# Attention and ternary MLP in one kernel: the comparison of the weights moved to Pool and ScalarE, the weights loaded earlier, and unread matrix passes in the first seam

## The chip, the cores and the metric

The kernel runs on one core of a Trainium2 chip. A core has TensorE (PE, the matrix engine; its weight loads are shown as PEld), VectorE (DVE), ScalarE (ACT), GpSimd (POOL) and SyncE (SP), each with its own queue of instructions that it works off in order, and 16 DMA engines, which take the transfers that SP and ScalarE issue. The metric is the time of one execution on the device in microseconds (us). Less is better.

## The reference

The input `x` is 32 sequences of 256 tokens with 128 features. One layer of attention and one gated MLP follow, each with a residual and a layer norm:

```python
scores = einsum('bhid,bhjd->bhij', Q, K) / sqrt(8)          # 16 heads of 8
scores = where(j > i, -inf, scores) - (i - j)               # causal, with a linear decay
x = layernorm(x + softmax(scores) @ V @ Wo.T + bo)
h = silu(x @ w1.T * s1) * (x @ w2.T * s2)                   # 128 -> 512
h = gelu(h @ h1.T * sh1); h = gelu(h @ h2.T * sh2)          # 512 -> 512 -> 512
x = layernorm(x + h @ w3.T * s3)                            # 512 -> 128
```

All of it is float32. The weights of the MLP (`w1`, `w2`, `h1`, `h2`, `w3`) are random -1, 0 or 1, times 8. There are about 0.7 million of them, in 11 blocks of 128 x 512.

## The kernel before

**Pairs and steps.** The 32 sequences are worked off as 16 pairs (512 tokens each). `step(n)` (line 725) weaves three things into one stream: the attention of pair n, the score maxima of pair n+1, and (from step 1 on) the MLP of pair n-1. PE, DVE, ACT and SP keep the order in which the Python program calls them (`InOrder`, line 50), so the order of the lines is the order on each engine. POOL's instructions are placed by the scheduler.

**Projections and stacks.** `project(n)` (line 314) transposes `x`, and makes queries and keys. Each is kept as a rounded half and a rest (`halves`, line 295): ACT writes `qhi`, `khi` from PSUM in the fast matmul type, DVE writes `qlo`, `klo`. Eight transfers of 256 KB (`stack`, line 305: four for q, four for k) put these halves into the rows of `qs` and `ks`, so that one matmul over 62 or 64 rows gives a score with the precision of both halves, the decay and the causal cut. I call the eight transfers stack n. Before, `stack(0, "k")`, `stack(1, "k")` and `stack(2, "k")` are issued by ACT (lines 690, 697, 758), all others by SP.

**Score tiles.** `row_maxima(n, i)` (line 373, i from 0 to 11) fills one PSUM tile of 128x1024 scores on PE, and DVE reduces it to maxima `m`. `maxima_to_rows` (line 408) transposes maxima (`pm`), splits them (`mhi` on ACT, `mlo` on DVE) and sends them by small transfers on SP into two more rows of `qs`. The tiles `mhi` and `mlo` have one buffer each, so the second pair of them waits until the first has been sent. `weigh(n, i)` (line 430) then makes the scores again, less their maximum, ACT takes the exponential `e`, POOL clears what lies above the diagonal (line 463), and `outputs` multiplies with the values `vaug` (`pa`). Score tiles, weigh tiles and MLP tiles share three PSUM buffers (`two`, line 289); small results share two (`work`, line 286).

**Opening and steps 0 and 1.** The constant rows of `qs` and `ks` are filled, pairs 0 and 1 are projected and stacked (lines 684 to 697), the values of pair 0 are projected (line 698, `pv` on PE, `vaug` on DVE), and `wo` is loaded by ACT. Then come the 12 score tiles of pair 0 with the values of pair 1 and the first `maxima_to_rows` in the middle (lines 710 to 717), the load of the MLP weights on SP (line 714) and of the scales (line 718), and two score tiles of pair 1 (`LEAD`, line 719). Step 0 runs the 12 weigh tiles of pair 0 beside the other ten score tiles of pair 1 and the projection of pair 2. Its tail, `rest()` (line 761), is the seam to step 1: the last outputs, the values of pair 2, `finish` (`pon`, `onT`, `po`).

**The comparison of the weights.** The MLP has a fast form for weights that the fast matmul type holds exactly, and a slow one for others. `inexact_weights` (line 622) copies each of the 11 blocks into the fast type on ACT (`near`), compares copy and original on DVE with an accumulated count (`differ`, `found`), and adds the counts with one matmul (`pcount`). One block is done in each of the first 11 tiles of step 0 (line 743). All engines load the number after step 0 and branch on it (lines 810 to 826); these inputs take the fast form.

**Waits of transfers.** In the order of the built instructions the transfers of SP and ACT share eight semaphores in turn. An issue waits until the transfer that used its semaphore before, mostly the eighth before it, has landed.

Of the kernel before, what the change touches and what calls it, by code (L numbers as in the profile page):

```python
# [17 lines left out]
P = 128  # L18
# [43 lines left out]
def tile_attn_ffn(  # L62
# [47 lines left out]

    qs = [const.tile([P, W, TOK], F32R, name=f"qs{i}") for i in range(2)]
    ks = [const.tile([P, W, TOK], F32R, name=f"ks{i}") for i in range(2)]
    sctx = ctx.enter_context(ExitStack())
    setup = sctx.enter_context(tc.tile_pool(name="setup", bufs=1))

# [69 lines left out]
    def fill(dst, nm, eng, groups=slice(0, W)):  # L185
        t, base = fills[nm]
        to = dst[:, groups, :]
        t = t.unsqueeze(1).to_broadcast([P, groups.stop - groups.start, TOK])
        if eng is act:
            act.activation(to, t, AF.Identity, bias=base)  # L190
        else:
            eng.tensor_scalar(to, t, base, None, ALU.add)
# [34 lines left out]
    for i in range(2):  # L227
# [7 lines left out]


    layers = (
        ("w1", w1T, 1, HID), ("w2", w2T, 1, HID), ("h1", h1T, KC, HID), ("h2", h2T, KC, HID),
        ("w3", w3T, KC, D),
    )  # L240
    near = {
        nm: const.tile([P, k, o], F32R, name=f"{nm}_near") for nm, _, k, o in layers
# [3 lines left out]
        sc[nm] = const.tile([P, KC], F32, name=nm)  # L246
    sc["s3"] = const.tile([P, 1], F32, name="s3")

    def load_layers(pool):
        got = {}  # L250
        for nm, src, k, o in layers:
            got[nm] = pool.tile([P, k, o], F32, name=f"{nm}_sb")
            sp.dma_start(out=got[nm], in_=src.rearrange("(k p) o -> p k o", p=P))
        return got
# [31 lines left out]
    def work(nm):  # L286
        return ps_w.tile([P, 512], F32, name=nm, tag="work")

    def two(nm):
        return ps_s.tile([P, 2, 512], F32, name=nm, tag="s")  # L290
# [4 lines left out]
    def halves(n, ps, bias, nm):  # L295
        pool = setup if n == 1 else hlp
        hi = pool.tile([P, TOK], F32R, name=f"{nm}hi_{n}", tag=f"{nm}hi")
        act.activation(hi, ps, AF.Identity, bias=bias)
        lo = pool.tile([P, TOK], F32R, name=f"{nm}lo_{n}", tag=f"{nm}lo")
        vec.scalar_tensor_tensor(  # L300
            lo, ps, bias, hi.bitcast(F32), ALU.add, ALU.subtract
        )
        return hi, lo

    def stack(n, nm, eng=sp):
        for r, part in {
            "q": ((0, 0), (1, 0), (2, 1), (3, 1)), "k": ((0, 0), (2, 0), (1, 1), (3, 1))
        }[nm]:
            eng.dma_start(
                out=pairs[n][nm][PAIRING + r :: W, :, :].bitcast(F32),  # L310
                in_=pairs[n][nm + "s"][part].bitcast(F32),
            )
# [26 lines left out]
    def project_values(n):  # L339
        xT, v = pairs[n]["xT"], vaug[n % 2]  # L340
        pairs[n]["v"] = v
        pv = work(f"pv_{n}")
        for t in range(NT):
            pe.matmul(
                pv[:, t * D : (t + 1) * D], lhsT=xT[:, t * P : (t + 1) * P], rhs=wv_sb,
                start=True, stop=True,
            )
        to = v[:, :, 0 : H // 2 * VSLOT].rearrange("p t (r c k) -> p t r c k", r=2, c=C)
        src = pv.rearrange("p (t r e c d) -> p t r e c d", t=NT, r=2, e=2, c=C)
        bias = bv_sb.rearrange("p (r e c d) -> p r e c d", r=2, e=2, c=C)  # L350
        for r in range(2):
            for e in range(2):
                vec.tensor_tensor(
                    to[:, :, r, :, 2 * e * VHEAD : 2 * e * VHEAD + HD], src[:, :, r, e],
                    bias[:, r, e].unsqueeze(1).to_broadcast([P, NT, C, HD]), ALU.add,
                )
# [265 lines left out]
    def inexact_weights():  # L622

        found = const.tile([P, 11], F32, name="found")
        at = 0
        for nm, *_ in layers:
            rows = [t[nm].rearrange("p k o -> p (k o)") for t in (loaded, near)]
            for c in range(0, rows[0].shape[1], HID):
                whole, part = (t[:, c : c + HID] for t in rows)
                act.copy(part, whole)  # L630
                differ = once.tile([P, HID], F32, name=f"differ_{at}", tag="differ")
                vec.scalar_tensor_tensor(
                    differ, whole, 1.0, part.bitcast(F32), ALU.mult, ALU.not_equal,
                    accum_out=found[:, at : at + 1],
                )
                at += 1
                yield
        ones_col = const.tile([P, 1], F32, name="ones_col")
        nc.gpsimd.memset(ones_col, 1.0)
        count = work("pcount")  # L640
        pe.matmul(count[0:1, 0:11], lhsT=ones_col, rhs=found, start=True, stop=True)
        total = const.tile([1, 1], F32, name="total")
        vec.tensor_reduce(total, count[0:1, 0:11], AX.X, ALU.add)
        number = const.tile([1, 1], I32, name="number")
        vec.tensor_copy(number, total)
        pairs["inexact"] = number
# [32 lines left out]
    def run(gen):  # L679
        for _ in gen:  # L680
            pass


    ahead = project(0)
    next(ahead)
# [2 lines left out]
    run(ahead)  # L688
    stack(0, "q", sp)
    stack(0, "k", act)  # L690
    fill(ks[1], "k", act)
    ahead = project(1)
    next(ahead)
    fill(qs[1], "q", vec)
    run(ahead)
    stack(1, "q", sp)
    stack(1, "k", act)
    project_values(0)
    for a in range(G):
        act.dma_start(  # L700
            out=wo_sb[C * HD * a : C * HD * (a + 1), :],
            in_=woT[:, :, a, :].rearrange("c d o -> (c d) o"),
        )
    sctx.close()
    ep = enter(tc.tile_pool(name="ep", bufs=5))
    op = enter(tc.tile_pool(name="op", bufs=2))
    yp = enter(tc.tile_pool(name="yp", bufs=2))
    lctx = ctx.enter_context(ExitStack())
    once = lctx.enter_context(tc.tile_pool(name="once", bufs=1))
    for i in range(6):  # L710
        row_maxima(0, i)
    project_values(1)
    maxima_to_rows(0, (0,))
    loaded = load_layers(once)
    for i in range(6, 3 * G):
        row_maxima(0, i)
    maxima_to_rows(0, (1,))
    load_scales()
    for i in range(LEAD):
# [5 lines left out]
    def step(n, exact=None, ws=None, hp=None, gp=None):  # L725


        side = iter(())
        settling = (
            last(n - 2, exact, ws, gp) if n > 1 else first_norm(0) if n else inexact_weights()  # L730
        )
        ahead = project(n + 2) if n + 2 < NPAIR else iter(())
        for i in range(3 * G):
            weigh(n, i)
            j = i + {0: LEAD, 1: -LAG}.get(n, 0)
            if n + 1 < NPAIR and 0 <= j < 3 * G:
                row_maxima(n + 1, j)
            if i == 3 and late:
                run(late.pop())
            next(side, None)  # L740
            if n and i == 9:
                turn(n - 1, exact)
            if i in ((0, 2) if n > 1 else (0, 2, 4, 6)) if n else i < 11:
                next(settling, None)

            if i in ((3, 4, 5) if n == 1 else (1, 3, 5)):
                next(ahead, None)
            if i % 3 == 2:
                run(side)
                side = outputs(n, i // 3)  # L750
            if n == 0 and i == 3 * G - LEAD:
                maxima_to_rows(1)
        if n < 2:
            run(settling)
        run(ahead)
        if n + 2 < NPAIR:
            stack(n + 2, "q")
            stack(n + 2, "k", sp if n else act)


        def rest():
            for _ in range(3):
                next(side)
                yield
            if n == 1:
                for i in range(3 * G - LAG, 3 * G):
                    row_maxima(2, i)
                    yield
            if 0 < n < NPAIR - 1:
                maxima_to_rows(n + 1)  # L770
            run(side)
            yield
            if n + 2 < NPAIR:
                project_values(n + 2)
                yield
            last_steps = finish(n)
            next(last_steps)
            yield
            yield from last_steps
            if n:  # L780
                yield
                yield from first_norm(n)
            if n == NPAIR - 1:
                yield
                turn(n, exact)
            if n > 1:
                next(settling)
                late.append(settling)

        if n:  # L790
            prepare(AF.Silu)
        due = rest()
        for _ in feed(n - 1, exact, ws, hp, gp) if n else ():
            next(due, None)
        run(due)
# [85 lines left out]
```

## Time and profile before

| what | value |
|---|---|
| time, median of 3 runs (lowest to highest) | 823.96 us (823.79 to 824.07) |
| the profiled execution's own time | 824.06 us |
| its span, first to last instruction | 822.2 us |
| PE busy | 784.6 us (95%) |
| DVE, ACT, POOL busy | 636.0, 527.5, 260.8 us |
| mean granted clock of PE | 0.98 |
| PE busy from 0 to 22 us, 22 to 42.8, 42.8 to 71, 71 to 82 | 11.71, 17.89, 26.03, 6.16 us |
| PE busy from 100 to 810 us | 703.50 of 710 us |
| DMA from 10 to 32 us | 205 to 208 GB/s, mean share of its 16 engines 0.91 to 1.00 |

A timeline row reads: start, duration, engine, line, operation, tile written <- tiles read, shapes, number of instructions merged in the row, and in brackets the idle time of the engine before it with what ended it. Most rows show line 58, because all engines but POOL are called through `InOrder`; tiles tell them apart. SPq and ACTq are issues of transfers by the queues of SP and ACT. The duration of several merged rows runs from the first start to the last end. The windows view gives for each stretch the busy time of each engine, the mean granted clock of PE (PEclk, 1.00 is full), the share of time in which the DMA engines were busy, and what they moved. The chip records the clock only from its first change on; before 32.3 us the view shows 1.00 though no record lies there, and the matmuls of the score tiles last as long (0.80 us for four) as later at 0.50.

### The profile page before, as it was taken

Reading aid. Unit: us, or ns where it says so; the run is one execution under the profiler, and the core shown is the slowest. Engines: PE = TensorE matmul, PEld = TensorE weight load, DVE = VectorE, ACT = ScalarE, POOL = GpSimd, SP = SyncE. Lnnn points to the kernel's source line nnn. Section 1 sums busy time; section 2 is a strip of 40 time slices with the busy share of each in tenths; the row PEclk is TensorE's granted clock in tenths of the full one; section 3 lists DMA queues with packets and bytes.
Section 4 is the critical chain, followed back from the end, with each engine's and each line's share of the span. In section 5 each row is a group of like instructions: output and inputs, shape, how many; then the busy total and the mean of one; then the engine's idle time right before and its main releaser. Section 6 shows DMA issues by size and latency. Waiting matters only on the chain.

```text
span 822.2 us, 17431 instructions
## 1 busy us (share of the span) xinstructions
PE 784.6 (95%) x7046; PEld 555.8 (68%) x7046; DVE 636.0 (77%) x1247; ACT 527.5 (64%) x719; POOL 260.8 (32%) x341
## 2 busy tenths in 40 slices
PE   4896999999999999999999999999999999999994
PEld 2664676776767677676767767676767767666673
DVE  6786778877887887778788877888878787873674
ACT  5065556766666766766576676667666666758572
POOL 5033413333142333414232342424243231424211
PEclk9879999999999999999999999999999999999998
DMA  6824140403204140410404040130404022000001
GB/s 147 213 62 106 29 92 14 106 15 74 60 14 106 28 107 14 92 42 21 110 17 106 27 101 20 43 90 15 107 26 104 4 62 59 14 4 14 1 8 37
DMA packets 39898, 47.49 MB, mean 58 GB/s; under 512 B 3968, under 2 KB 21632, under 8 KB 39808
## 3 DMA queue, kind: packets, MB, share of 16 engines
q1 hardware_dynamic: 37152, 42.82, 22.0%
q10 hardware_dynamic: 2656, 3.48, 1.9%
q8 instruction: 57, 0.93, 0.5%
q14 instruction: 33, 0.27, 0.1%
HBM read 7.48 MB, written 4.19 MB: 14 GB/s over the span
## 4 chain that ended last, share of the span: by engine, by line
PE 83%; DVE 4%; ACT 3%; issue 1%; DMA 0%; POOL 0%; ACTq 0%; POOLq 0%; DVEq 0%
PE peven L58 14%; PE podd L58 14%; PE s L58 12%; PE pa L58 11%; PE pw L58 10%; PE s_2d L58 2%; PE s_3d L58 2%; PE po L58 2%; PE s_0d L58 2%; PE s_1d L58 2%; PE pt L58 2%; PE pv L58 2%; PE pk L58 2%; PE pq L58 2%; PE px1T L58 1%; PE py L58 1%
## 5 line engine op out<-in xcount | busy, mean ns | idle before, releaser
L58 DVE TENSOR_REDUCE m<-s 128x4 f32<-128x1024 f32 x128 | 155.5, 1218 | 14.6 <-PE s L58 13.3
L58 ACT ACTIVATE e<-s 128x1024 f32<-128x1024 f32 x128 | 130.7, 1022 | 44.2 <-PE s L58 34.2
L463 POOL TENSOR_SCALAR_AFFINE_SELECT e<-e 128x512 f32<-128x512 f32 x128 | 82.6, 646 | 218.5 <-ACT e L58 189.3
L58 PE MATMUL podd<-h,h_near 128*128 128x512 f32 x512 | 131.3, 403 | 1.0 <-DVE m L58 0.5
L58 PE MATMUL peven<-hodd,h_near 128*128 128x512 f32 x512 | 122.7, 396 | 0.0
L58 PEld LDWEIGHTS peven<-hodd,h_near 128*128 128x128 f32 x512 | 95.7, 187 | 23.4 <-DVE hodd L58 0.3
L58 PEld LDWEIGHTS podd<-h,h_near 128*128 128x128 f32 x512 | 91.8, 188 | 23.1 <-DVE h L58 3.2
L58 ACT ACTIVATE hodd<-podd,sh 128x512 fp32r<-128x512 f32 x64 | 44.0, 688 | 62.7 <-PE podd L58 62.6
L58 PE MATMUL pw<-x1T,w_near 128*128 128x512 f32 x256 | 75.6, 418 | 1.1 <-DVE h0w L58 1.1
L274 POOL TENSOR_TENSOR rsa<-rsa,half 128x4 f32<-128x4 f32 x16 | 16.3, 1018 | 176.7 <-DVE rsa L58 176.7
L58 DVE SCALAR_TENSOR_TENSOR h0w<-pw,s,sg 128x512 f32<-128x512 f32 x64 | 47.9, 748 | 30.4 <-ACT sg L58 30.4
L58 PEld LDWEIGHTS s<-qs,ks 64*128 64x128 f32 x512 | 38.9, 188 | 47.7 <-issue 34.1
L58 PE MATMUL pa<-e,vaug 128*32 128x256 f32 x1024 | 70.6, 389 | 0.0
L58 PE MATMUL s<-qs,ks 64*128 64x256 f32 x512 | 65.3, 335 | 0.6 <-ACT e L58 0.5
L58 DVE TENSOR_TENSOR heven<-evenw,heven 128x512 fp32r<-128x512 f32 x64 | 44.2, 692 | 26.6 <-ACT evenw L58 26.1
L58 ACT ACT_TABLE_LOAD x47 | 60.3, 1283 | 3.4 <-issue 2.6
L58 ACT ACTIVATE sg<-pw,s 128x512 f32<-128x512 f32 x64 | 43.7, 684 | 28.2 <-PE pw L58 27.9
L58 PE MATMUL s<-ks,qs 62*128 62x256 f32 x512 | 56.9, 302 | 2.4 <-ACT e_0d L58 1.8
L58 ACT ACTIVATE heven<-peven,sh 128x512 fp32r<-128x512 f32 x48 | 33.4, 696 | 39.8 <-PE peven L58 39.8
L58 PEld LDWEIGHTS pw<-x1T,w_near 128*128 128x128 f32 x256 | 43.4, 188 | 18.4 <-ACT nothing L58 5.8
L581 POOL TENSOR_TENSOR h<-h0w,h 128x512 fp32r<-128x512 f32 x31 | 40.0, 1291 | 43.5 <-DVE h L58 41.2
L58 DVE TENSOR_TENSOR hodd<-oddw,hodd 128x512 fp32r<-128x512 f32 x64 | 43.7, 684 | 10.0 <-ACT oddw L58 9.9
(147 smaller groups left out, 1418.1 us busy)
## 6 DMA issues: line engine op xcount, KB each, us to landing
qs<-qhi SPq DMA_DIRECT2D x32, 256.0 KB
qs<-qlo SPq DMA_DIRECT2D x32, 256.0 KB
ks<-khi SPq DMA_DIRECT2D x26, 256.0 KB
ks<-klo SPq DMA_DIRECT2D x26, 256.0 KB
x<-in_x_dram SPq DMA_DIRECT2D x16, 256.0 KB
out_dram<-z SPq DMA_DIRECT2D x15, 256.0 KB
ks<-khi ACTq DMA_DIRECT2D x6, 256.0 KB
ks<-klo ACTq DMA_DIRECT2D x6, 256.0 KB
```

What stands on the lines that cost most here:

```text
L58: return lambda *args, **kw: self.tc.keep_in_program_order(call(*args, **kw))
L274: nc.gpsimd.tensor_tensor(rs, rs, half[:, 0:NT], ALU.pow)
L463: nc.gpsimd.affine_select(out=on_diagonal, in_=on_diagonal, pattern=[[0, on_diagonal.shape[1]], [1, P]], base=0, channel_multiplier=-1, co ...
L581: (nc.gpsimd if o < (1 if final else 2) else vec).tensor_tensor(h[:, 1, o, :], whole, h[:, 0, o, :].bitcast(F32), ALU.subtract)
```

## The change

1. *Weights loaded earlier.* `load_layers` is called right after stack 0 (before: after the first `maxima_to_rows`), in the order `w1`, `w2`, `w3`, `h1`, `h2`. On SP the five transfers (2.9 MB) now stand before the third `x` and before stack 1. The pools `ep`, `op`, `yp` and `once` are opened before the pool `setup`, so that the weights have room while it is open.
2. *Comparison on POOL and ACT.* Each block is copied by ACT as before; POOL then subtracts the copy in place, and ACT adds up the magnitudes of the rest (`Abs` with an accumulated sum), one block later. DVE only turns the 11 sums into "not zero". Three blocks are done after the projection of pair 1, two among the first six score tiles, six among the last six; the last sum stands at tile 5 of step 0, and the count (`pcount`) at tile 8.
3. *Two score tiles ahead.* Score tiles 0 and 1 of pair 0 come right after the projection of pair 1. The rests `qlo`, `klo` of pair 1 are held back (`due`) until their reduces stand in DVE's order. `project_values(0)` moves from before the score tiles to just before `project_values(1)`.
4. *Issues of ACT given to SP.* `stack(1, "k")`, the load of `wo` and `stack(2, "k")` are issued by SP.
5. *Unread passes.* `warm(4)` makes four matmuls of a 128x128 bf16 identity with 512 columns into a score buffer that nobody reads. It stands before the second `maxima_to_rows` of pair 0, and four times in the tail of step 0: after the first half of the last `pa`, after the second, after `pt`, and before `po`.

```diff
@@ line 237
-        ("w1", w1T, 1, HID), ("w2", w2T, 1, HID), ("h1", h1T, KC, HID), ("h2", h2T, KC, HID),
-        ("w3", w3T, KC, D),
+        ("w1", w1T, 1, HID), ("w2", w2T, 1, HID), ("w3", w3T, KC, D), ("h1", h1T, KC, HID),
+        ("h2", h2T, KC, HID),
@@ halves, line 300
-        vec.scalar_tensor_tensor(
-            lo, ps, bias, hi.bitcast(F32), ALU.add, ALU.subtract
+        due.append(
+            lambda: vec.scalar_tensor_tensor(lo, ps, bias, hi.bitcast(F32), ALU.add, ALU.subtract)
         )
+        if n != 1:
+            run_due()
@@ inexact_weights, line 630
+        def add_up(rest, total):
+            act.activation(rest, rest, AF.Abs, accum_out=total)
...
                 act.copy(part, whole)
-                differ = once.tile([P, HID], F32, name=f"differ_{at}", tag="differ")
-                vec.scalar_tensor_tensor(
-                    differ, whole, 1.0, part.bitcast(F32), ALU.mult, ALU.not_equal,
-                    accum_out=found[:, at : at + 1],
-                )
+                nc.gpsimd.tensor_tensor(whole, whole, part.bitcast(F32), ALU.subtract)
+                left.append((whole, found[:, at : at + 1]))
+                if at:
+                    add_up(*left.pop(0))
                 at += 1
                 yield
+        add_up(*left.pop())
+        yield
...
+        vec.tensor_scalar(found, found, 0.0, None, ALU.not_equal)
@@ new, before line 684
+    def warm(count):
+        t = two("warm")
+        for i in range(count):
+            pe.matmul(
+                t[:, i % 2, :], lhsT=ident_b, rhs=ident_b.unsqueeze(1).to_broadcast([P, NT, P]),
+                start=True, stop=True,
+            )
@@ opening, line 690
     stack(0, "k", act)
+    loaded = load_layers(once)
     fill(ks[1], "k", act)
...
     run(ahead)
+    for i in range(2):
+        row_maxima(0, i)
+    run_due()
     stack(1, "q", sp)
-    stack(1, "k", act)
-    project_values(0)
+    stack(1, "k", sp)
+    comparison = inexact_weights()
+    for _ in range(3):
+        next(comparison)
     for a in range(G):
-        act.dma_start(
+        sp.dma_start(
...
-    for i in range(6):
+    for i in range(2, 6):
         row_maxima(0, i)
+        if i > 3:
+            next(comparison)
+    project_values(0)
     project_values(1)
     maxima_to_rows(0, (0,))
-    loaded = load_layers(once)
     for i in range(6, 3 * G):
         row_maxima(0, i)
+        next(comparison)
+    warm(4)
     maxima_to_rows(0, (1,))
@@ step, line 734
             weigh(n, i)
+            if n == 0 and i == 5:
+                next(comparison)
+            if n == 0 and i == 8:
+                run(comparison)
...
-            stack(n + 2, "k", sp if n else act)
+            stack(n + 2, "k")
@@ rest, line 762
             for _ in range(3):
                 next(side)
+                if n == 0:
+                    warm(4)
                 yield
...
             next(last_steps)
+            if n == 0:
+                warm(4)
             yield
```

More of the change, by code (lines that the diff above doesn't have):

```diff
@@ L112, in tile_attn_ffn @@
     ks = [const.tile([P, W, TOK], F32R, name=f"ks{i}") for i in range(2)]
+    ep = enter(tc.tile_pool(name="ep", bufs=5))
+    op = enter(tc.tile_pool(name="op", bufs=2))
+    yp = enter(tc.tile_pool(name="yp", bufs=2))
+    lctx = ctx.enter_context(ExitStack())
+    once = lctx.enter_context(tc.tile_pool(name="once", bufs=1))
     sctx = ctx.enter_context(ExitStack())
@@ L247, in tile_attn_ffn, with load_layers @@
     sc["s3"] = const.tile([P, 1], F32, name="s3")
-    def load_layers(pool):
+    def load_layers(pool, some=layers):
         got = {}
-        for nm, src, k, o in layers:
+        for nm, src, k, o in some:
             got[nm] = pool.tile([P, k, o], F32, name=f"{nm}_sb")
@@ L299, in halves, with run_due @@
         lo = pool.tile([P, TOK], F32R, name=f"{nm}lo_{n}", tag=f"{nm}lo")
-        vec.scalar_tensor_tensor(
-            lo, ps, bias, hi.bitcast(F32), ALU.add, ALU.subtract
-        )
+        due.append(
+            lambda: vec.scalar_tensor_tensor(lo, ps, bias, hi.bitcast(F32), ALU.add, ALU.subtract)
+        )
+        if n != 1:
+            run_due()
         return hi, lo
+    due = []
+    def run_due():
+        while due:
+            due.pop(0)()
     def stack(n, nm, eng=sp):
@@ L624, in inexact_weights @@
         found = const.tile([P, 11], F32, name="found")
-        at = 0
+        at, left = 0, []
+        def add_up(rest, total):
+            act.activation(rest, rest, AF.Abs, accum_out=total)
         for nm, *_ in layers:
@@ L704, in tile_attn_ffn @@
     sctx.close()
[L705 to L709, printed above, removed]
-    for i in range(6):
+    for i in range(2, 6):
         row_maxima(0, i)
+        if i > 3:
+            next(comparison)
+    project_values(0)
     project_values(1)
     maxima_to_rows(0, (0,))
-    loaded = load_layers(once)
     for i in range(6, 3 * G):
         row_maxima(0, i)
+        next(comparison)
+    warm(4)
     maxima_to_rows(0, (1,))
@@ L729, in step @@
         settling = (
-            last(n - 2, exact, ws, gp) if n > 1 else first_norm(0) if n else inexact_weights()
+            last(n - 2, exact, ws, gp) if n > 1 else first_norm(0) if n else iter(())
         )
@@ L742, in step @@
                 turn(n - 1, exact)
-            if i in ((0, 2) if n > 1 else (0, 2, 4, 6)) if n else i < 11:
+            if i in ((0, 2) if n > 1 else (0, 2, 4, 6)):
                 next(settling, None)
```

## The prediction

> **What bounds the kernel now.** The slices and section 4 of the page say that nearly the whole span is TensorE (PE busy 95%, 83% of the chain). The change touches only what lies before that: the first 82 us. So I read stage by stage there: the timeline for what starts when, then the table of windows for the limit of each stretch. I call score tile (n,i) what `row_maxima(n, i)` makes, and weigh tile (n,i) what `weigh(n, i)` makes.
>
> The opening, in the timeline:
>
> ```profile
> 19.22 0.75 DVE L58 SCALAR_TENSOR_TENSOR qlo<-pq,bq_sb,qhi 128x512 fp32r<-128x512 f32 x1 [4.01 <-ACT qhi L58]
> ...
> 22.03 0.79 PE L58 MATMUL s<-ks,qs 62*128 62x256 f32 x4
> ...
> 22.20 0.89 DVE L58 TENSOR_TENSOR vaug<-pv,bv_sb 128x128 f32<-128x128 f32 x4 [1.57 <-issue]
> ...
> 23.13 2.36 DVE L58 TENSOR_REDUCE m<-s 128x4 f32<-128x1024 f32 x2
> ...
> 38.60 1.20 DVE L58 TENSOR_REDUCE m<-s_3d 128x8 f32<-128x1024 f32 x1
> ...
> 39.86 1.01 PE L58 MATMUL pm<-ident,m 128*8 128x128 f32 x4 [1.92 <-DVE m L58]
> ```
>
> From 23.13 to 39.80 VectorE goes from reduce to reduce, and PE waits for the last: VectorE is the limit. The work that the change puts between the reduces (`qlo`, `vaug`) stands before 23.13 here, beside idle time.
>
> The windows (columns: window; its length; PE, PEld, DVE, ACT, POOL busy; granted clock; DMA share; GB/s):
>
> ```profile
> 10.00:21.00 11.00, 5.87 (x12) 2.87 (x13) 6.07 (x7) 5.42 (x4) 5.52 (x8) 1.00 0.91 205
> ...
> 40.80:50.90 10.10, 10.10 (x81) 7.60 (x80) 8.93 (x12) 6.14 (x9) 4.47 (x7) 0.50 0.44 137
> ...
> 52.80:62.50 9.70, 9.70 (x132) 6.04 (x128) 7.93 (x15) 8.12 (x12) 3.01 (x4) 1.00 0.01 3
> 69.00:80.50 11.50, 7.67 (x78) 5.88 (x78) 4.70 (x20) 2.72 (x5) 1.38 (x2) 0.85 0.85 190
> 80.50:81.80 1.30, 0.00 (x1) 0.03 (x2) 0.53 (x1) 1.30 (x2) 1.30 (x3) 1.00 0.00 0
> 101.50:111.00 9.50, 9.50 (x72) 6.43 (x71) 7.45 (x12) 6.16 (x9) 3.67 (x3) 1.00 0.99 221
> ```
>
> Step 0 (42.8 to 71) is PE's: 10.10 of 10.10 at half clock, then 9.70 of 9.70 at full clock until 62.5. VectorE, which the comparisons load, has slack there; it holds PE only from 62.5 to 69. The seam to step 1 belongs to a transfer:
>
> ```profile
> 68.08 1.42 ACTq L58 DMA_DIRECT2D ks<-khi  x2
> ...
> 70.73 2.91 SPq L58 DMA_DIRECT2D qs<-qhi  x2
> ...
> 81.80 0.50 PE L58 MATMUL s<-ks,qs 62*128 62x256 f32 x4 [1.78 <-ACT e_0d L58]
> ```
>
> The view names `e_0d`, but that tile's buffer was not wanted. Score tile (2,0) needs all eight transfers of pair 2's stack (2.1 MB); the DMA moves 190 GB/s up to 80.5 (2.19 MB) and then nothing, and 1.3 us later the tile starts.
>
> **Opening: +1.7.** Stack 0 is 2.1 MB of the 2.26 MB moved from 10 to 21, and the third `x` shares its end, so it is there at about 21.5. I bound the first score tile by 20.2 (2.1 MB at 205 GB/s from 10.0) and today's 22.03, and take 21.5, 0.53 earlier. In the changed order two reduces precede `qlo` and `klo` of pair 1 (0.67 apart: 1.34), and pair 0's `vaug` (0.89) follows the first six reduces. All are now inside the VectorE chain: 1.34 + 0.89 - 0.53 = +1.7 at the last reduce, at `pm` and at weigh tile (0,0). It is +0.4 if the stack is early.
>
> What lies beside it: the 11 Pool subtractions have no row; the nearest is `h<-h0w,h` on Pool (128x512, 1.29 us), below it a 128x512 select (0.65), above it four 128x128 additions (4 x 0.43 = 1.7). The sums of magnitudes on ScalarE lie between 0.57 (a 128x512 copy) and 1.02 (128x1024). With 1.29 and 0.68, the chain of copies, subtractions and sums that stands before the second `mhi` on ScalarE frees it at about 42.1, and `pm` ends at about 42.5: hidden, at nothing; at 1.7 a subtraction six of them cost 2.5, some +2. Second cover: on SP's queue the weights (2.9 MB; the window from 34 to 45 moved them at 267 GB/s, 10.8 us) and the third `x` (0.26 MB, 1.0) now precede stack 1, so from 20.5 on stack 1 starts at about 32 and, at 9.5 us a stack (2.1 MB at 221 GB/s), lands at about 41.5 to 42. Score tile (1,0) wants it at 42.5; the first `mhi` and `mlo`, queued behind it, are wanted by the second `mhi` and `mlo` at the same time. Cost nothing, but each us of delay counts in full. The four passes before the second `pm` (no row; `podd` has 0.25 a 128x512 pass at full clock, 0.5 at half) take 1.0 to 2.0 and stand beside the last two reduces (2.3).
>
> **Clock: +0.85.** The granted clock changes at 35.7, 52.8, 73.3, 76.7, 83.5 and 86.9 (from its mean in short windows): always a multiple of 3.41 apart. It rises at 52.8, right after the first `pa` (50.90, 1.93 long, 128 rows). Score and weigh tiles (62 or 64 rows) kept PE busy for 10 us and did not raise it. Moved by 1.7, `pa` runs 52.6 to 54.5, past that tick, and the next is 56.2: `pq` then runs at half clock (2.04 instead of 1.12) and step 0 is at 56.4 where it was at 53.82. Bounds 0 and 1.7 (half a period).
>
> [...]
>
> **End of step 0: -1.0.** With the comparisons (11 of 0.68 to 0.80) gone from VectorE, the last reduce of pair 1 follows its tile. From 62.5 on: PE waits about 0.5 for the moved `pcount`; tile (1,11) ends at 64.25, the reduce 64.75 to 65.95 (65.48 to 66.70 before), `pm` 66.15, second-half `mlo` done 68.0 (68.93 before). SP's first stack issue goes from 70.73 to 69.75.
>
> **Seam: +0.4.** All eight transfers of stack 2 now wait on SP behind the four of the maxima; `ks` started on ScalarE's queue at 68.08 before. SP alone has a row: pair 3's stack, first issue 100.42, last bytes 110.9. Plus 1.0 until the tile starts (1.3 in the seam; 0.6 if no DMA engine lags) is 11.5 from first issue to tile; before it was 81.80 - 70.73 = 11.07. So +0.4, between 0 and +0.7. `oT` starts 1.1 earlier, without ScalarE's issues, `pv` and `po` run at full clock, and weigh tile (1,0) follows `pa` by about 5.7 (`oT` 0.65, passes 0.35 past it, `pt` 0.66, `rec` and `on` 1.3, the rest of `pv` and `vaug` 1.4, `onT` 0.69, `po` 0.6) instead of 6.9 us. That saves nothing while score tile (2,0) waits for the stack: weigh tiles and their exponentials are done about 2.5 us after (1,0), some 3 us before it. The 16 passes there (1.0 per four) lie in the same slack.
>
> [...]
>
> **Sum.** 1.7 + 0.85 - 1.0 + 0.4 = +2.0 at score tile (2,0). From there PE is the limit to the end, so it stays. The profiled execution took 824.06 (span 822.2 and 1.86 around it): 826.06; the median of the runs, 823.96, is 0.1 lower, so **826.0**. A measurement of this kernel can tell 0.2% (1.65 us) from no change.
>
> **Rivals.**
> - *Faster: the passes raise the clock at 42.6 and it holds through step 0.* VectorE is the limit then: from 43.8, 12 reduces (1.22), `xT`, `qlo`, `klo`, `rec`, `on` = 17.7, so the last reduce ends near 61.5 instead of 66.7 and stack 2 follows: -5.3, 818.7; if it holds for part of the way, 819 to 822. For: four 128-row passes and `pm` nearly fill 39.1 to 42.6. Against: before, from 32.3 to 35.7, score tiles alone let it fall again. It decides from the point where the clock is still 1.0 at 46 to 50. 0.18.
> - *Even: the opening costs nothing or the clock rises at its old tick* (stack 0 earlier than 21.5; or `pa` still in time). 2.0 - 1.3 or 2.0 - 0.85: about 824.8, down to 822. For: the clock's ticks may lie otherwise. 0.17.
> - *Slower still: stack 1 or the comparison chain ends after `pm`* (+1 to +2), or score tile (2,0) is late enough that the clock misses 86.9 (+1.7). 828 to 830. For: both covers above are under 1 us. 0.15.
> - Forecast, 824.8 to 828: 0.50, of which 0.10 lie within 0.2%.
>
> Faster by over 0.2%: 0.18 and 0.06 of the even case, 0.24. Within: 0.11 and 0.10, 0.21. Slower: 0.40 and 0.15, 0.55. The range leaves out the lower part of the first rival (0.07) and most of the last (0.13): 820.0 to 828.0.
>
> **What would show it.** First reduce near 22.6 and last of pair 0 near 41.5; clock 0.50 until 56.2; first stack issue on SP after the four maxima near 72.3; no DMA for a us before score tile (2,0) at about 83.8; from 100 us on the same table. Wrong, if VectorE has idle time before 40, if the clock is up in 44 to 52, or if score tile (2,0) starts as soon as its PSUM buffer is free.

## The result, and two profiles of the changed kernel

The changed kernel takes 826.62 us (median of 7 runs, 822.07 to 829.30) against 823.96 (823.25 to 824.53): 1.0027 times the time before, 95% interval 1.0016 to 1.0039. The forecast was 826.0.

One thing has to be read first: the profiled execution took 822.07 us, the fastest of the seven and 2.0 less than the profiled one of before. A trace of one execution can stand at the edge of the distribution. So the same kernel was profiled again (first experiment below, 826.40 us, near the median), and both traces are read here, the first as "the 822 trace", the second as "the 826 trace".

Timeline of the 822 trace, the rows that answer to those of before:

```profile
23.09 2.36 DVE L58 TENSOR_REDUCE m<-s 128x4 f32<-128x1024 f32 x2 [7.99 <-PE s L58]
...
40.76 1.20 DVE L58 TENSOR_REDUCE m<-s_3d 128x8 f32<-128x1024 f32 x1
...
42.02 1.01 PE L58 MATMUL pm<-ident,m 128*8 128x128 f32 x4
...
68.64 1.23 SPq L58 DMA_DIRECT2D qs<-qhi  x2
...
80.17 0.80 PE L58 MATMUL s<-ks,qs 62*128 62x256 f32 x4 [2.50 <-ACT e L58]
```

Timeline of the 826 trace:

```profile
22.97 2.36 DVE L58 TENSOR_REDUCE m<-s 128x4 f32<-128x1024 f32 x2 [7.90 <-PE s L58]
25.24 0.74 DVE L58 SCALAR_TENSOR_TENSOR qlo<-pq,bq_sb,qhi 128x512 fp32r<-128x512 f32 x1
...
31.41 0.89 DVE L58 TENSOR_TENSOR vaug<-pv,bv_sb 128x128 f32<-128x128 f32 x4 [0.24 <-issue]
...
40.78 1.20 DVE L58 TENSOR_REDUCE m<-s_3d 128x8 f32<-128x1024 f32 x1
...
42.04 1.01 PE L58 MATMUL pm<-ident,m 128*8 128x128 f32 x4
...
53.08 1.93 PE L58 MATMUL pa<-e,vaug 128*32 128x256 f32 x16
...
72.08 1.23 SPq L58 DMA_DIRECT2D qs<-qhi  x2
...
83.67 0.80 PE L58 MATMUL s<-ks,qs 62*128 62x256 f32 x4 [2.54 <-ACT e L58]
```

Up to `pm` the two are the same: the first reduce starts where it did before (23.13), `qlo`, `klo` and `vaug` now stand between reduces, and the last reduce starts 2.2 later (38.60 before). After `pm` they part by 3.4 us. The windows say why (behind the five busy columns stands the granted clock). First the 822 trace, then the 826 trace:

```profile
43.81:53.81 10.00, 9.26 (x122) 6.01 (x121) 8.46 (x9) 5.15 (x6) 4.56 (x8) 1.00 0.15 34
53.81:63.51 9.70, 9.37 (x138) 6.16 (x132) 8.19 (x14) 7.14 (x10) 4.08 (x5) 1.00 0.01 2
68.64:79.90 11.26, 7.77 (x72) 5.41 (x67) 5.58 (x21) 4.36 (x5) 2.30 (x4) 0.91 0.85 189
79.90:80.17 0.27, 0.00 (x0) 0.03 (x1) 0.27 (x1) 0.00 (x0) 0.27 (x1) 0.50 0.00 0
```

```profile
43.81:54.87 11.06, 11.06 (x92) 7.59 (x92) 8.33 (x8) 4.09 (x4) 4.65 (x8) 0.50 0.15 30
54.87:64.57 9.70, 9.37 (x126) 5.70 (x122) 6.58 (x9) 7.05 (x10) 2.99 (x4) 1.00 0.01 2
72.08:83.40 11.32, 7.76 (x72) 5.41 (x67) 5.64 (x21) 4.36 (x5) 2.36 (x4) 0.95 0.85 188
83.40:83.67 0.27, 0.00 (x0) 0.03 (x1) 0.27 (x1) 0.00 (x0) 0.27 (x1) 0.50 0.00 0
```

In the 822 trace the clock rose at 43.81, just after the four passes and `pm`, and held; in the 826 trace it stayed at 0.50 until 54.87, and PE was busy for all of the time from 43.81 on.

The difference to before at six stations tells where time comes and goes. Starts on PE or SP; (2,i) is score tile i of pair 2:

| trace | second `pm` of pair 0 | weigh tile after first `pq` | `pm` of pair 1 | first issue of stack 2 on SP | (2,0) | (2,3) |
|---|---|---|---|---|---|---|
| before | 39.86 | 53.82 | 66.75 | 70.73 | 81.80 | 91.02 |
| forecast | +1.7 | +2.55 | +1.95 | +1.6 | +2.0 | +2.0 |
| 822 trace | +2.16 | -1.28 | -1.78 | -2.09 | -1.63 | -1.13 |
| 826 trace (e1) | +2.18 | +2.17 | +1.66 | +1.35 | +1.87 | +2.60 |
| e2 without the first four passes | +2.21 | +3.16 | +2.88 | +2.57 | +3.75 | +4.84 |
| e3 without the passes of the seam | +2.33 | +2.35 | +1.84 | +1.53 | +2.58 | +3.21 |
| e4 without passes | +1.45 | +2.04 | +1.53 | +1.22 | +2.38 | +3.13 |
| e5 = e4, k of stack 2 by ACT | +1.93 | +2.88 | +2.53 | +2.75 | +2.09 | +2.10 |
| e6 = e4, old opening | -0.09 | +0.87 | +0.37 | +0.07 | +1.09 | +2.14 |
| e9 = e4, comparison on DVE | +2.23 | +2.16 | +2.17 | +2.34 | +2.60 | +2.63 |
| e10 clock held | +0.22 | -2.70 | -3.20 | -2.85 | -1.72 | -0.17 |
| e11 before, clock held | +0.11 | -2.78 | -2.78 | -2.26 | -3.24 | -3.32 |

What stands in the last column is carried to about 800 us unchanged (within 0.1); the last 20 us add -0.9 to +0.2. In the 822 trace VectorE's last row is 1.18 ahead of before (815.03 for 816.21) and the span is 1.84 shorter, so there the difference comes behind that row.

### The profile page after: what moved, and what is told of

Same layout as the page of the kernel before. It is cut to its first block, busy times and chain, and to the rows that moved or that the text cites. A ratio compares the mean times of both kernels' runs of the same rounds, so it can differ in the third digit from the quotient of the medians.

```text
span 820.3 us, 17476 instructions
## 1 busy us (share of the span) xinstructions
PE 784.0 (96%) x7066; PEld 553.4 (67%) x7066; DVE 629.0 (77%) x1226; ACT 535.4 (65%) x741; POOL 272.8 (33%) x352
## 4 chain that ended last, share of the span: by engine, by line
PE 86%; DVE 6%; ACT 4%; issue 1%; DMA 1%; POOL 0%; SPq 0%; POOLq 0%; ACTq 0%; DVEq 0%
PE peven L58 14%; PE podd L58 14%; PE s L58 12%; PE pa L58 12%; PE pw L58 10%; PE s_1d L58 2%; PE s_2d L58 2%; PE s_3d L58 2%; PE s_0d L58 2%; PE pv L58 2%; DVE m L58 2%; PE po L58 2%; PE pt L58 2%; PE pk L58 2%; PE pq L58 2%
```

## The experiments

Theory A: three things of the changed kernel's own make the difference (longer opening, earlier end of step 0, later stack 2), and where the grid of the clock falls decides from run to run. Rival B: the transfers do. By grid I mean the times of the clock's changes: in the 822 trace they stand at 9.68, 13.09, 16.51, 19.92, 33.57, 36.99, 43.81, 77.95, 84.77 and 815.23, multiples of 3.41 us apart, as those of before do; what sets them no trace here shows. Each time is a median; ratios are to runs of the kernel before on the same chip (medians of 824.00 for e1 to e4, 823.66 for e5 to e8, 824.50 for e9 to e11, 823.87 for e12). Where runs of different chips are compared, each counts from its own before; e4 is +3.18.

**e1, e2, e3, e4: the unread passes.** e1 is the changed kernel. The others take out lines:

```diff
 e2, e4:
-    warm(4)
     maxima_to_rows(0, (1,))
 e3, e4, in rest(), both places:
-                if n == 0:
-                    warm(4)
```

> The changed kernel once more, unaltered, to see another of its executions in a trace. Theory A: what a run takes hangs on where the 3.41-us grid of the clock falls on the four passes before the second maxima and the matmuls after them: if one grid window is filled with them the clock is up from about 44 us and stays up (about 822), else it comes up only after the first pa, at 54 to 58 (826 to 829). Then the median is again 825 to 828, the runs spread by 4 us or more, and a profiled execution of more than 825 has the clock at 0.50 until 54 or later. Theory B: the spread comes from the transfers (weights ahead of stack 1, stack 2 by SP alone): a profiled execution of more than 825 has the clock up at 44 as in the first trace and a landing of stack 1 or of stack 2 that is 2 us or more later in its stage.

> The four passes before the second maxima are left out, the four times four in the seam stay. Theory A: the clock never comes up before the first pa, so every run is one of the late ones: median 826 to 828, spread under 3 us, clock 0.50 until 54 or later in the trace. Theory B: the passes do nothing: median within 0.5 us of the changed kernel's and the same spread of 5 to 7 us.

> The sixteen passes in the seam to step 1 are left out, the four before the second maxima stay. My prediction had them in slack, at nothing: median within 0.7 us of the changed kernel's, the spread of 5 us or more stays (theory A: it comes from the first four). A rival: the passes in the seam decide when the clock is up at the start of step 1, so the time without them is 1 to 3 us more.

> All unread passes are left out: what is left is the reordering, the comparison on POOL and ACT, and the issues by SP. Theory A: like the run without the first four, 826 to 828 with a spread under 3 us; this is then the change without the lucky runs, +2 to +4 over the kernel before. Theory B: within 0.5 us of the changed kernel, same spread.

| run | us (lowest to highest, runs) | ratio (95%) |
|---|---|---|
| e1 | 826.40 (825.07 to 827.45, 7) | 1.0030 (1.0019 to 1.0041) |
| e2 | 828.02 (826.39 to 828.23, 5) | 1.0042 (1.0029 to 1.0055) |
| e3 | 826.82 (822.23 to 831.27, 12) | 1.0033 (1.0016 to 1.0051) |
| e4 | 827.18 (827.03 to 827.98, 5) | 1.0042 (1.0029 to 1.0054) |

Of 26 runs with the first four passes (changed kernel, e1, e3), three took 822.1 to 823.0 and the others 825.1 or more; of ten without them none took less than 826.4. That is what theory A says, but three of 26 against none of ten can also be chance, e1's spread was 2.4, not 4, and only the first of the three was traced. The traces say more. Here are the 3.41 us of the grid in which most of the second `pm` lies, in the 822 trace, in e2 and in e1 (where they are counted back in steps of 3.41 from the rises at 57.49 and 54.87):

```profile
40.40:43.81 3.41, 3.31 (x16) 1.27 (x14) 1.70 (x3) 2.34 (x6) 2.39 (x2) 0.50 0.01 2
```

```profile
40.42:43.83 3.41, 1.76 (x12) 0.95 (x12) 1.69 (x3) 2.36 (x6) 2.40 (x2) 0.50 0.01 2
```

```profile
41.22:44.63 3.41, 3.31 (x18) 1.49 (x16) 1.70 (x3) 1.54 (x4) 1.58 (x2) 0.50 0.01 2
```

The 822 trace and e2 have the grid and `pm` (42.02 and 42.07) in the same place, and the four passes are what differs there: with them the clock rose at the end of the window, without them it did not. e1 has the passes, but its grid stands 0.8 later, so that 0.7 of their 1.89 us lie in the window instead of 1.5. PE is busy as long (3.31), more of it with tiles of 62 and 64 rows, and the clock did not rise. That the clock made the other two early runs is inferred. Without these passes the clock came at 57.49 in e2:

```profile
43.81:57.49 13.68, 13.68 (x98) 8.63 (x100) 8.36 (x8) 4.50 (x5) 4.65 (x8) 0.50 0.11 25
```

The passes of the seam change nothing that can be told in the time (826.82 against 826.40), as predicted.

e4 showed something else: stack 2 takes 12.2 us from SP's first issue to tile (2,0), in e1 11.6. The lists of queues from 71.9 to 84 us, while the stack is under way (queue and kind: packets, MB, share of the time of the 16 engines), e1 and then e4:

```profile
q1 hardware_dynamic: 1172, 2.13, 79.4%
```

```profile
q1 hardware_dynamic: 1172, 2.13, 76.8%
q8 instruction: 1, 0.02, 0.7%
```

In e4 a 16 KB packet of instructions is moved in this stretch (0.7% of the engines' time, some 1.4 us), and e2's list has one too (0.7%, 12.25 from issue to tile). In e1 the list has none, and in the 822 trace the packet came before the first issue (67.42, issue 68.64), and there it is 11.5 to 11.6. So all twenty passes together may have moved it out of the way, some 0.65 us of their worth. That the packet costs this is not shown: before, one lies inside the stack as well (from 72.96, for 1.32 us), and the tile comes 11.07 after SP's first issue, with ACT issuing too.

**e5: the k transfers of stack 2 given back to ACT** (on e4).

```diff
-            stack(n + 2, "k")
+            stack(n + 2, "k", sp if n else act)
```

> The changed kernel without passes (827.2, lowest 827.0, highest 828.0), and with the four k transfers of stack 2 given back to ACT. My seam step: they start some 2 us earlier, score tile (2,0) comes about 11.1 us after SP's first issue of stack 2 instead of 12.2, so -0.5 to -1: 826.2 to 826.7. The rival, a rate of the DMA engines that does not ask who issues: within 0.3 us of 827.2, and the last landing where it was.

825.52 us (823.88 to 828.08, 12 runs), 1.0023 (1.0012 to 1.0035): +1.86, 1.3 less than e4, with intervals that overlap a little (e4's begins at 1.0029).

```profile
70.61 1.43 ACTq L58 DMA_DIRECT2D ks<-khi  x2
72.14 2.46 ACTq L58 DMA_DIRECT2D ks<-klo  x2
73.48 1.30 SPq L58 DMA_DIRECT2D qs<-qhi  x2
```

ACT begins 2.9 us ahead of SP, and tile (2,0) starts at 83.89, 10.4 after SP's first issue instead of 12.2. The gain, 1.3 in the medians and 1.8 in the trace, is larger than I expected (0.5 to 1); the mechanism is the one of my seam step. Whether the packet of instructions has a part in it is not shown. The rate is the same (188 GB/s by SP alone in the 826 trace, 190 before by both); what the tile gains is the time of issue.

**e6: the old order of the opening** (on e4).

```diff
-        if n != 1:
-            run_due()
+        run_due()
...
-    for i in range(2):
-        row_maxima(0, i)
-    run_due()
     stack(1, "q", sp)
     stack(1, "k", sp)
+    project_values(0)
...
-    for i in range(2, 6):
+    for i in range(6):
...
-    project_values(0)
     project_values(1)
```

> The changed kernel without passes, and with the old order of the opening: no score tiles ahead of pair 1, the rests qlo and klo made at once, the values of pair 0 before the score tiles; weights, comparison and issues stay as changed. My opening step (two rests and the values inside VectorE's chain cost 1.5 to 2.2): last reduce of pair 0 back at 39.8, pm at 39.9, first weigh tile at 42.8, time 825.0 to 825.7. The rival, that the weights ahead of stack 1 are what costs: the first score tile of pair 1 then waits for stack 1 beyond 41.5 and the time stays within 0.5 us of 827.2.

825.33 us (824.43 to 826.55, 11 runs), 1.0017 (1.0008 to 1.0026): +1.67, 1.5 less than e4.

```profile
39.77 1.01 PE L58 MATMUL pm<-ident,m 128*8 128x128 f32 x4 [1.44 <-DVE m L58]
```

`pm` is back, and the first weigh tile too (42.68), with the weights still ahead of stack 1. The time is as expected, and the rival is out: the order of the opening costs, not the transfers. A run with e5 and e6 together and no passes was not made, so that their gains add up is not shown.

**e7, e8: single passes to hold the clock.** In the traces of before, of the changed kernel and of e2 to e4 the clock rose between 31.5 and 34.7 us, after the values, and fell 3 or 7 us later (before at 1.00 from 32.31 to 35.72, the 822 trace from 33.57 to 36.99; the mean from 36 to 40 is 1.00, 0.76 and 0.80 in e2, e3 and e4, from 40 to 44 it is 0.55, 0.50 and 0.50). e7 is e4 with one pass (`hold()`, 128x512 into a small PSUM buffer) behind each of the last six score tiles of pair 0 and the first four weigh tiles; e8 has the edits of e5 and e6 as well. Row activity in the expectations from here on is an estimate: PE's busy time in a stretch of a trace, weighted by the rows in use of 128.

```diff
     for i in range(6, 3 * G):
         row_maxima(0, i)
+        hold()
         next(comparison)
...
             weigh(n, i)
+            if n == 0 and i < 4:
+                hold()
```

> The changed kernel with its passes taken out and single ones (one 128x512 pass into one of the small PSUM buffers) put behind each of the last six score tiles of pair 0 and behind the first four weigh tiles of step 0. Theory A: the clock came up at 32 to 36 us in every trace and fell again; with the passes each 3.41-us window holds more row activity than the 0.42 to 0.56 at which it stayed in the lucky run, so it stays up from there through step 0: first stack issue near 68.5, 821.0 to 822.5, all runs within 2.5 us. The rival: passes behind score tiles delay the tiles that VectorE waits for, or do not hold the clock: 827 to 830.

> The three last edits at once: k of stack 2 by ACT, the old order of the opening, the single passes that hold the clock. If the three are worth what I say and add up (-0.7, -2.0, -5.2 from 827.2): 819 to 820.5, faster than both kernels, first weigh tile near 41.8. If the clock does not hold: 824 to 825.

e7: 829.45 us (828.36 to 829.71, 5 runs), 1.0058 (1.0045 to 1.0071). e8: 828.40 (826.75 to 832.01, 6 runs), 1.0062 (1.0043 to 1.0080). Theory A failed in e7, where the rival's range holds, and both ranges failed in e8. The clock was at 1.00 from 34.20 to 41.03 in e7 and up to 41.7 in e8, and it fell when PE had waited for the last reduce before `pm` (2.00 and 2.13 us); then the four passes in step 0 take 0.54 each (45.76 to 46.30 in e7) on a PE that is the limit at half clock (busy 19.38 of the 20.48 us from 41.03). The windows of e8 (the first column after the length is PE):

```profile
38.40:41.70 3.30, 1.93 (x22) 1.26 (x24) 2.00 (x4) 2.11 (x6) 2.16 (x2) 1.00 0.09 25
41.75:55.40 13.65, 13.46 (x85) 7.65 (x84) 7.71 (x7) 4.10 (x4) 4.66 (x8) 0.50 0.11 25
```

**e9: the comparison on VectorE again** (on e4, in the first eleven tiles of step 0).

```diff
-                nc.gpsimd.tensor_tensor(whole, whole, part.bitcast(F32), ALU.subtract)
-                left.append((whole, found[:, at : at + 1]))
+                vec.scalar_tensor_tensor(
+                    differ, whole, 1.0, part.bitcast(F32), ALU.mult, ALU.not_equal,
+                    accum_out=found[:, at : at + 1],
+                )
```

> The changed kernel without passes, and with the comparison of the weights on VectorE in the first eleven tiles of step 0, as before the change; early weights, opening and issues stay as changed. My step for the end of step 0 (-1.0 predicted; the traces so far show the delay at the last reduce of pair 1 smaller by 0.6 to 0.9 than at the start of full clock): this gain goes, so 827.8 to 828.2 against 827.2. The rival: VectorE had slack all along and the delay is won back by something else: within 0.3 us of 827.2.

828.23 us (826.57 to 830.14, 6 runs), 1.0054 (1.0037 to 1.0071): +3.73, 0.55 more than e4, with intervals that overlap. The table settles what the time leaves open: with the comparison on VectorE the delay stays at +2.16 from the first `pq` to the `pm` of pair 1 and is +2.34 at SP's first issue; without it it falls from +2.04 to +1.22 (e4) and from +2.17 to +1.35 (826 trace).

**e10, e11: the gap before `pm` filled.** e10 is e8, e11 the kernel before with the passes of e8 and nothing else; both have six more passes:

```diff
+    for _ in range(6):
+        hold()
     maxima_to_rows(0, (1,))
```

> The run with all three edits, with six more single passes between the last score tile of pair 0 and the second pm, where its trace lost the clock (window 38.3 to 41.8, row activity 0.37, PE idle 2.1 us before pm). Theory A: the clock then stays up from 31 to 35 us through step 0, last reduce of pair 1 near 62, first stack issue of SP near 66, 818.5 to 821, spread under 3 us. The rival: the clock falls in the first windows of step 0 in any case, as VectorE sets the pace and leaves PE too little: 825 or more.

> The kernel before the change, with the same passes (one behind each of the last six score tiles of pair 0, six before the second pm, one behind each of the first four weigh tiles), and nothing else. Comparison still on VectorE: from 43.8 its work in step 0 is 17.7 plus 11 comparisons of 0.7 to 0.8, 25.9, so its last reduce cannot come before 66.5 or so even at full clock: 823.5 to 825, no gain. The rival, that the clock alone sets step 0: 819 to 820.5.

e10: 822.26 us (820.08 to 826.34, 12 runs), 0.9980 (0.9963 to 0.9998). e11: 820.80 (818.93 to 830.12, 12 runs), 0.9978 (0.9953 to 1.0002). Now the clock holds, in e10 to 69.23, in e11 to 66.42. Still e10 missed its range, with a spread of 6.3 instead of under 3, and the interval of e11 reaches 1.0002, so its 3.7 us stand at the edge of the noise. The same two windows in e10:

```profile
38.40:41.70 3.30, 2.37 (x24) 1.18 (x22) 1.91 (x3) 2.32 (x6) 2.37 (x2) 1.00 0.15 34
41.75:55.40 13.65, 13.12 (x148) 7.95 (x148) 10.93 (x11) 7.79 (x10) 6.24 (x10) 1.00 0.11 25
```

Both are 2.7 to 2.8 ahead of before when step 0 is under way. e10 then gains 0.5 more at the `pm` of pair 1, where e11 does not: in e11 VectorE is the limit (the third busy column of its windows):

```profile
42.50:52.80 10.30, 9.77 (x116) 5.99 (x117) 10.30 (x17) 7.50 (x11) 5.55 (x8) 1.00 0.27 73
52.80:63.00 10.20, 10.13 (x148) 6.43 (x146) 10.16 (x20) 9.20 (x14) 4.83 (x6) 1.00 0.01 2
```

My expectation for e11 failed although VectorE is the bound: I let its work start at 43.8 and put all eleven comparisons before the last reduce. It starts at 41.83, two comparisons come after, and consecutive rows overlap by some 0.08. e10 loses its lead in the seam:

```profile
66.41 3.59 ACTq L58 DMA_DIRECT2D ks<-klo  x2
70.09 0.59 ACT L58 COPY oT<-pa 128x512 f32<-128x512 f32 x1 [4.21 <-DMA qs<-mhi]
...
70.73 1.11 PE L58 MATMUL pt<-ident,oT 128*128 128x128 f32 x4 [3.00 <-ACT oT L58]
```

ACT's issue of `klo` is held for 3.6 us, `oT` stands behind it, PE idles, the clock falls at 69.23 and is up again only at 86.30. So these issues by ACT hold up ACT's own work, which part 4 of the change avoids. SP for these issues, together with a held clock, was not tried.

**e12: more passes on the kernel before.** e11 with eight instead of six passes, two behind each of the first two weigh tiles, and five in the wait for (2,0):

```diff
+            if n == 1 and j == 0:
+                for _ in range(5):
+                    hold()
             if n + 1 < NPAIR and 0 <= j < 3 * G:
```

> The kernel before with the passes of the last-named run and more where its trace had the weakest windows: eight instead of six before the second pm, two instead of one behind the first two weigh tiles, and five in the wait for the first score tile of pair 2 (76.7 to 80.1, row activity 0.34, after which its clock fell). If the clock decides: all or nearly all runs between 817.5 and 821, median 818.5 to 820.5, and the clock at 1.00 past the first score tile of pair 2. If more passes only add work for PE, which was at 1.00 of each window from 46 us on: 821 to 823.

820.61 us (818.80 to 825.26, 12 runs), 0.9972 (0.9954 to 0.9991). The interval lies below 1, so this beats both kernels. In its trace the clock is at 1.00 past (2,0), as meant (window from (2,0) on):

```profile
79.34:88.10 8.76, 8.09 (x86) 4.43 (x88) 7.60 (x9) 3.90 (x6) 6.17 (x10) 1.00 0.11 32
```

The median is 0.1 above the expected range, and the spread did not shrink: four of twelve runs took 823.4 to 825.3. What they lost was not traced.

## Why the forecast came close, step by step

Read on the 826 trace, whose time is 2.34 above the profiled one of before (forecast +2.0; the medians differ by 2.66):

- *Opening, +1.7 forecast, +2.18 measured* (+1.45 to +2.33 in e1 to e5 and e9). The two rests (1.32 from 25.24 to 26.56) and `vaug` (0.89) went into VectorE's chain as said, and e6 took them out again. The term that failed is the -0.53: I let the tile start at 21.5, as soon as stack 0 is there. Before, the last transfer of the stack landed at 21.36 and the tile started at 22.03, behind `pv`, so the work ahead did hold it. In the 822 trace the transfer lands at 21.69, with the loads of the weights now behind it, and the tile starts 0.30 after that, at 21.99, with nothing else ahead of it. So the tile now waits for the transfer, and 0.04 was won (0.15 in the 826 trace); the first reduce starts at 22.97 to 23.16 in e1 to e4 (23.13 before).
- *"From reduce to reduce" was too strong.* VectorE is idle for 1.35 of the 16.67 us from the first reduce to the end of the last before, and for 1.57 of 19.01 in the 826 trace, where it waits for `pv` and `mhi`. So idle time before 40, which I named as a sign of being wrong, tells nothing: the kernel before has it too.
- *Covers of the opening.* POOL's subtraction takes 1.27 (nearest row 1.29). The sum of magnitudes takes 0.63 and 0.19 more for reading the accumulator, against 0.68. The chain stayed hidden beside the reduces, and so did the four passes (1.89 at half clock) and stack 1.
- *Clock, +0.85 forecast, 0 to +0.95 measured.* The changes lie multiples of 3.41 us apart in the 822 trace as in before, but where they stand against the program differs from one execution to the next (rises at 43.81 in the 822 trace, at 54.87 in the 826 trace, of the same kernel; three times 3.41 after 43.81 would be 54.05). In the 826 trace 54.87 came in time (step 0 +2.17, as the opening left it), in e2, e5 and e6 it cost 0.95, in e4 0.59. A single value was the wrong form for this term.
- *End of step 0, -1.0 forecast, -0.82 measured* (+2.17 to +1.35). e9 shows that it is the comparison.
- *Seam, +0.4 forecast, +0.52 measured,* and between +0.26 (e9) and +1.2 (e2) in the other traces with SP alone. e5, where ACT issues again, has -0.66, so the cost comes with the issue by SP alone; why it differs so much between the traces is open.
- *After (2,0), 0 forecast, +0.47 measured in the time,* +0.5 to +1.1 at (2,3). I had this only in the third rival. Before, the clock was down from 83.51 to 86.92, and (2,0) itself ran at full clock. In the 822 trace it is down twice as long, from 77.95 to 84.77, and (2,0) starts inside, as it starts at half clock in e1 to e6 but e5: 0.79 to 0.80 where it took 0.50, `pa` 1.93 where it took 1.14. My reading is that a later stack lets PE idle long enough to lose the clock; e11 and e12 fit it: without passes in that wait (PE idle for 2.02) the mean clock from 78.56 to 88.00 is 0.82 and `pxT` takes 1.12, with five it is 1.00 from 79.34 to 88.10 and `pxT` takes 0.66. Lateness alone does not settle it: in e9 the tile is as late (+2.60) and runs at full clock (0.50), and the `pa` after it takes 1.61.

So the sum is near for reasons that partly cancel: clock 0.85 too much, opening 0.5 and the cold tile 0.5 too little. The steps are the ones I named, but that the sum came so near is in part luck.

*The first rival,* for which I gave 0.18, came true in the profiled run, and in at most 3 of the 26 runs with the first four passes. Its condition (clock 1.0 at 46 to 50), which is also one of my signs of being wrong, is met there, yet it brought 2.0, not 5.3. I had made VectorE the limit through step 0; its rows fill 8.46 of the first 10.00 us and 8.19 of the next 9.70, PE 9.26 and 9.37: the two wait for each other.

*What raised the clock.* A busy PE alone did not: the 826 trace has it busy 11.06 of 11.06 us from 43.81 at 0.50, most of that with tiles of 62 and 64 rows. So the forecast was right to trust the row from 40.80 to 50.90 (10.10 of 10.10 at 0.50). And the four passes were too few: 1.89 us of passes and 1.01 of `pm` came before a rise in the 822 trace, where 1.5 of the passes lie in the last 3.41 us before it, and before none in e1, where 0.7 do. That the rows of the matmuls and the place of the grid decide is my reading of these traces; no run varied either alone. What holds it is open too: in e10 it stayed at 1.00 behind 3.30 us with PE busy for 2.37 (38.40 to 41.70), in e7 it fell behind 3.41 us with PE busy for 2.51 (37.62 to 41.03).

## What to carry to other kernels

Where the clock rises at different places in two executions of one kernel (43.81 and 54.87 here), price it as two outcomes and look at several executions: one trace can be the fastest of seven. Work that raises the clock paid in most runs only where it bridged the waits until PE is steadily busy: 25 short passes in the waits of the old kernel won 3.3 us in the median (e12), though a third of the runs stayed late, while with four in one place of the changed kernel only three of 26 executions were early. Before an instruction is moved into a chain of reduces, ask whether the chain's start was held by that instruction or by a transfer, and when the transfer will land in the new order.

## What the runs showed of the hardware that was not expected

- A 16 KB packet of instructions takes 0.88 to 1.57 us (57 of them in before, 57 in the 822 trace). Where it falls differs between the traces: 1.2 us before SP's first issue of stack 2 with all twenty passes (822 trace), inside the stack with none (e4). Where the list from 71.9 to 84 us has it, the tile comes 12.2 and 12.25 after the issue (e4, e2), where it has none 11.5 and 11.6 (822 trace, e1); before has one inside and takes 11.07, with ACT issuing too, so the cause is open.
- An unread 128x512 pass in a row of four takes 0.26 at full clock (four in 1.04, 822 trace) and 0.47 at half (four in 1.89).
- PE busy for 3.31 of 3.41 us stood before a rise of the clock in the 822 trace (43.81) and before none in e1 (44.63); in e1 more of it went to tiles of 62 and 64 rows.
- On ScalarE an accumulated sum has a second instruction of 0.19 behind its 0.63 (822 trace, 11 of each).
